# Two-layer graph convolution: raw gathers issued with the degree count's steps, and own-row products moved one group of sums earlier

## The chip, the cores and the metric

The kernel runs on one core of a Trainium2 chip. A core has a matrix engine (PE, with its weight loads shown as PEld), a vector engine (DVE), a scalar engine (ACT), a general engine (POOL, which here issues the indirect gathers) and SP, whose queue issues the plain loads and stores. All of them run side by side and wait for one another through semaphores. The metric is the device time of one execution in microseconds; smaller is better.

## The reference

The input is a table `x` of 6250 rows with 512 values, and 100000 edges `src -> dst` sorted by `dst`. Two Chebyshev convolutions run over it, with float32 throughout:

```python
deg  = segment_sum(ones(E), src, N)                 # how often a node is a source
dinv = where(deg > 0, rsqrt(max(deg, 1)), 0)
norm = -dinv[src] * dinv[dst]
conv = lambda h, W0, W1, b: h @ W0 + segment_sum(h[src] * norm[:, None], dst, N) @ W1 + b

h = relu(layernorm(x))
h = layernorm(conv(h, W1_0, W1_1, b1)) * gamma + beta
h = where(h >= 0, h, 0.01 * h)
out = x + conv(h, W2_0, W2_1, b2)
```

Each convolution thus needs, for every edge, the 512 values of its source row (2 KB), summed over the edges of one destination. `h @ W0` is called the own-row product below; the other product is that of the sums.

## The kernel before

**Chunks, units, groups, blocks.** The edges are cut into 782 chunks of 128 edges. Three chunks make a unit and four units a group, so a group of sums is 12 chunks; there are 66 groups in a layer, and group 0 has only one unit. The nodes are cut into 49 blocks of 128 rows. A chunk is gathered by one indirect DMA on POOL: 128 rows of 2 KB by the column of source indices `sidx[:, t]`. PE then multiplies it by a 0/1 selection matrix (`sel`, made by DVE in `choose`), which sums the edges of equal destination (`sums`, line 706), and ACT copies the group's sum to `agg` (line 721). Since the edges are sorted, a block's sums lie in about three successive groups. `inside[i]` names them, and `inside[i].stop` is the group in whose turn block `i` is finished. For the first blocks these stops are 3, 4, 6, 7, 8, 10, 11, 12, 14: three blocks for every four groups.

**Finishing a block.** `turn` (line 829) transposes the block's own rows `h` (`own`, line 596, four transposes, and an ACT copy to `hT`, line 598), places the groups' sums into the block (`place`, line 742) and scales them into `an` with ACT (line 841). `first_half` (line 845) transposes `an`, has DVE copy it to `aT` (line 851), and meanwhile does the own-row products from `hT` into a new PSUM tile `u_ps` (line 608). `second` (line 859) adds the products of the sums from `aT` and calls `finish`: on DVE a layer norm in layer 0 and a few sums in layer 1 (lines 804 to 824), then the store. Up to group 53 `second` of a block waits in the list `left` until the next group's turn. `hT` has one buffer; `u_ps` and `hT_ps` have two each.

**Order.** In the main loop (lines 932 to 1078) the instructions of PE, POOL and SP are issued in the order in which the code has them. Those of DVE and ACT are put in order by a planner. On PE a group's turn reads: `second` of the block left over, `own`, `place`, the sums of the group, `first_half`.

**Slots.** A gathered chunk lies in a slot until its sums are done. `ring` (line 46) gives the slots out: 12 are lent by the weights and biases, which arrive later, and 63 are the places where `x` lay; 8 of these go to later weights, so that from chunk 75 on 55 places are used in turn. Chunk 130 is therefore written to the slot of chunk 75, the first chunk of group 7, and its gather waits for the sums of group 7. All chunks after it have such a predecessor too.

**Before the main loop.** SP loads `x` (groups of 2, 4, 4, 4, 7, 7, 7, 7, 7 blocks) into the places. ACT takes the statistics and turns each block in place into `relu(layernorm(x))` (line 306), and SP stores it to a table in DRAM, `tab[0]` (line 307). A place is free for a gather when its block is stored. At the same time DVE and PE count the degrees: 25 steps `g` (line 379), in each of which DVE makes two one-hot tables `lo` and `hi` (line 382) for PE. Steps 1, 4, 7, 11, 17 and 21 also finish a part of the table (`turns`, line 355): 2, 4, 4, 4, 7 and 7 blocks. The first 76 chunks are gathered "raw", from `x` itself rather than from the table: 75 of them by `gather_raw` (line 268), of which the first 26 need no stored block (12 lent slots and 14 spare places), and the others one freed place each, in order. ACT scales raw chunks later (line 576), by factors that the `look_up` steps find.

Of the kernel before, what the change touches and what calls it, by code (L numbers as in the profile page):

```python
# [34 lines left out]
AHEAD_OF = 27  # L35
JOIN = 12
WIDE = 35
NARROW = 26
# [24 lines left out]
def gnn_kernel(  # L63
# [203 lines left out]

    def gather_raw(lo, hi):
        for t in range(lo, min(hi, X + RE + NB)):
            nc.gpsimd.indirect_dma_start(  # L270
                out=lent[t] if t < X else places[:, t - X, :D], out_offset=None, in_=x,
                in_offset=bass.IndirectOffsetOnAxis(ap=sidx[:, t : t + 1], axis=0))

    gather_raw(0, X + RE)

# [24 lines left out]
    def make_table(i0, n):  # L300

        for lo in range(i0, i0 + n, 2):
            hi = min(lo + 2, i0 + n)
            for i in range(lo, hi):
                v = places[:, RE + i, :D]
                nc.scalar.activation(v, v, AF.Relu, bias=nb_all[:, i : i + 1], scale=rs_all[:, i : i + 1])
            nc.sync.dma_start(tab[0][lo * P : hi * P, :].rearrange("(i p) d -> p i d", p=P),
                              places[:, RE + lo : RE + hi, :])
            gather_raw(X + RE + lo, X + RE + hi)

# [51 lines left out]
    with tc.tile_pool(name="deg", bufs=1) as dp, tc.tile_pool(name="onehot", bufs=2) as ohp, tc.tile_pool(  # L362
# [15 lines left out]
        for g in range(EJ // (2 * GJ)):  # L378
            hot = []
            for s, n, name in ((s_lo, LO, "lo"), (s_hi, HI, "hi")):  # L380
                t = ohp.tile([EP, GJ, n, 2], BF, name=name)
                nc.vector.tensor_tensor(  # L382
                    t, s[:, g * 2 * GJ : (g + 1) * 2 * GJ].rearrange("p (j s) -> p j s", s=2)[:, :, None, :]
                    .to_broadcast([EP, GJ, n, 2]),
                    iota_c[:EP, None, :n, :].to_broadcast([EP, GJ, n, 2]), op=OP.is_equal)
                hot.append(t.rearrange("p j n s -> p j (n s)"))
            k = turns.get(g)
            if k is not None:
# [63 lines left out]
def usual_path(tc, have):  # L452
# [19 lines left out]
    with ExitStack() as es:  # L472
# [273 lines left out]
        def end_matrices():  # L746
# [3 lines left out]
            nc.vector.tensor_scalar_add(at, iota_r[:, :r], 1.0 + END * P)  # L750
            ps = psum.tile([P, D], F32, name="u_ps")[:, :r]
            nc.tensor.matmul(ps, ones.to_broadcast([P, P]), own_row.pop(0)[:, :r], start=True, stop=True)
# [76 lines left out]
        def turn(layer, i, left=()):  # L829
# [4 lines left out]
            if i + AHEAD < NB:  # L834
                load(layer, i + AHEAD)
            hT = None if i in EARLY else own(layer, i)
            for k, aT in left:
# [7 lines left out]
        def first_half(layer, i, hT, an, between=None):  # L845
# [26 lines left out]
        def check():  # L872
# [12 lines left out]
            for at, num in ((1, min(D, NC - 1)), (1 + D, NC - 1 - D)):  # L885
                if num > 0:
                    ps = psum.tile([P, D], F32, name="u_ps")[0:1, :num]
                    nc.tensor.matmul(ps, ident[:, 0:1], dlx[:, at + 1 : at + 1 + num], start=True, stop=False)
# [17 lines left out]
            for j, (lo, hi) in enumerate(halves):  # L906
                up = pool.tile([P, D], F32, name="xt")[:, : P - 1]
                nc.vector.tensor_sub(up, ident[:, 1:], ident[:, : P - 1])
                ps = psum.tile([P, D], F32, name="u_ps")[: P - 1, : hi - lo]
                nc.tensor.matmul(ps, up, dlx[:, 1 + lo : 1 + hi], start=True, stop=True)  # L910
# [3 lines left out]
                yield  # L914
            ps = psum.tile([P, D], F32, name="u_ps")[0:1, 0:1]
            for j in range(2):
# [15 lines left out]
        for layer in range(2):  # L932
# [5 lines left out]
            for g in range(NS - 1):  # L938
# [469 lines left out]
```

## Time and profile before

| | |
|---|---|
| median of 3 runs | 2024.12 us (2021.15 to 2028.18) |
| profiled execution | 2021.31 us, of which the span from the first to the last instruction is 2019.4 us |
| granted TensorE clock, mean | 0.92 |
| PE busy | 1665.2 us, 82% of the span |
| POOL busy | 1489.1 us, 74% |
| DVE busy | 681.6 us, 34% |
| ACT busy | 389.0 us, 19% |
| DMA | 510.33 MB, 253 GB/s over the span |

A page of the profile shows one execution. It gives each engine's busy time, the groups of instructions by source line (count, mean length, and what ended the idle time before them), and the chain of work that ended last. Other views of the same trace list the instructions in order of time, sum the busy time of each engine in chosen stretches, or sum who waited for whom. In the last two, "issue" stands for time in which an engine waited for nothing that the profile shows. The releaser that is named is the last event before the start; where the idle time is the usual one between two instructions, that engine did not wait for it.

### The profile page before, as it was taken

The numbers are of one execution on the slowest core, as the hardware profiler recorded it, in microseconds if no ns is written. First come the engines' busy times: TensorE is split into PE (matmuls) and PEld (weight loads), VectorE is DVE, ScalarE is ACT, GpSimd is POOL, SyncE is SP. The second block draws the span as 40 slices with busy tenths as digits, with TensorE's granted clock in tenths as the row PEclk, the third lists the DMA queues.
The fourth block names the chain that finished last, engine by engine and source line by source line (L and its number), as shares of the span: only waits on it lengthen the run. The fifth ranks groups of instructions, "written<-read, shape, count | busy, mean of one in ns | idle before, by whom it ended". The sixth has DMA issues, their size and how long they took to land.

```text
span 2019.4 us, 19064 instructions
## 1 busy us (share of the span) xinstructions
PE 1665.2 (82%) x6850; PEld 663.2 (33%) x6850; DVE 681.6 (34%) x1454; ACT 389.0 (19%) x703; POOL 1489.1 (74%) x1578
## 2 busy tenths in 40 slices
PE   5589998677887776888888888888888888888898
PEld 4444443222333222333323322223322323333333
DVE  8975453323244233343352111122111211112221
ACT  7895221111111111111111011011010101011110
POOL 5477777777777777777777777777777777777774
PEclk9889999888998888999999999989999999989999
DMA  9998888887888887888877887787777778788875
GB/s 334 392 376 258 249 252 247 239 241 238 269 248 242 241 243 231 252 258 242 252 237 242 244 255 243 236 247 246 228 243 243 244 234 240 230 253 262 273 234 173
DMA packets 180278, 510.33 MB, mean 253 GB/s; under 512 B 33615, under 2 KB 35389, under 8 KB 180173
## 3 DMA queue, kind: packets, MB, share of 16 engines
q0 software_dynamic: 125120, 415.88, 68.5%
q1 hardware_dynamic: 55013, 93.12, 12.9%
q8 instruction: 56, 0.92, 0.2%
q14 instruction: 49, 0.40, 0.1%
q10 hardware_dynamic: 40, 0.02, 0.0%
HBM read 470.01 MB, written 38.86 MB: 252 GB/s over the span
## 4 chain that ended last, share of the span: by engine, by line
POOL 39%; PE 21%; DMA 17%; issue 16%; DVE 5%; ACT 2%; POOLq 0%; DVEq 0%; SPq 0%; ACTq 0%
POOL places L515 39%; DMA places<-tab,sidx 12%; PE u_ps L608 10%; PE ps L706 6%; PE an_ps L742 3%; DMA places<-tab,lidx 2%; ACT places L576 1%; DVE lo L382 1%; DVE hi L382 1%; PE hT_ps L849 1%; DMA dst_c<-in_dst_dram 1%; DMA places<-in_x_dram,sidx 1%; PE hT_ps L596 1%; DMA tab<-places 1%; DVE st L813 0%
## 5 line engine op out<-in xcount | busy, mean ns | idle before, releaser
L515 POOL DMA_INDIRECT places<-tab,sidx x1191 | 1130.1, 949 | 364.1 <-issue 327.5
L706 PE MATMUL ps<-places,sel 128*32 128x512 f32 x3104 | 511.0, 667 | 143.1 <-DMA places<-tab,sidx 86.6
L742 PE MATMUL an_ps<-agg,there 128*128 128x512 f32 (+1 forms) x554 | 268.6, 617 | 95.8 <-ACT agg L721 91.8
L515 POOL DMA_INDIRECT places<-tab,lidx x270 | 255.5, 946 | 82.3 <-issue 78.9
L706 PEld LDWEIGHTS ps<-places,sel 128*32 128x32 f32 x3104 | 102.0, 117 | 519.2 <-issue 194.6
L650 DVE TENSOR_TENSOR sel<-dlx,nodes_ps 128x384 f32<-128x384 f32 (+3 forms) x134 | 72.3, 541 | 417.5 <-PE ps L706 405.6
L608 PE MATMUL u_ps<-w,hT 128*128 128x512 f32 (+1 forms) x400 | 185.4, 607 | 20.7 <-ACT hT L598 20.2
L721 ACT ACTIVATE agg<-ps 128x512 f32<-128x512 f32 (+2 forms) x130 | 76.2, 588 | 610.0 <-PE ps L706 583.5
L608 PE MATMUL u_ps<-places,hT 128*128 128x512 f32 (+2 forms) x408 | 185.4, 598 | 2.9 <-ACT hT L598 2.9
L742 PEld LDWEIGHTS an_ps<-agg,there 128*128 128x128 f32 (+1 forms) x554 | 104.9, 197 | 216.8 <-issue 108.3
L608 PE MATMUL u_ps<-w,aT 128*128 128x512 f32 x384 | 173.1, 593 | 3.1 <-DVE aT L851 3.1
L608 PE MATMUL u_ps<-places,aT 128*128 128x512 f32 x384 | 173.4, 593 | 0.8 <-DVE aT L851 0.8
L690 DVE TENSOR_TENSOR sel<-sel,places 128x384 f32<-128x384 f32 (+9 forms) x76 | 35.1, 468 | 331.9 <-DMA places<-tab,sidx 331.9
L804 DVE SCALAR_TENSOR_TENSOR u_ps<-u_ps,root,bias 128x512 f32<-128x512 f32 x45 | 34.1, 758 | 284.8 <-PE u_ps L608 284.8
L598 ACT ACTIVATE hT<-hT_ps 128x512 f32<-128x512 f32 (+1 forms) x98 | 58.2, 594 | 291.3 <-PE hT_ps L596 290.9
L608 PEld LDWEIGHTS u_ps<-w,hT 128*128 128x128 f32 (+1 forms) x400 | 73.7, 194 | 96.7 <-issue 74.8
L608 PEld LDWEIGHTS u_ps<-places,hT 128*128 128x128 f32 (+1 forms) x408 | 75.7, 196 | 78.5 <-issue 73.6
L816 ACT ACTIVATE sd<-mv,eps 128x1 f32<-128x1 f32 (+1 forms) x49 | 14.4, 294 | 441.1 <-DVE mv L814 441.1
L270 POOL DMA_INDIRECT places<-in_x_dram,sidx x63 | 59.6, 947 | 52.6 <-ACT junk L286 19.0
L729 DVE TENSOR_SCALAR there<-iota_r,node_of 128x128 f32<-128x128 f32 (+1 forms) x286 | 68.2, 307 | 89.4 <-PE an_ps L742 89.4
L608 PEld LDWEIGHTS u_ps<-w,aT 128*128 128x128 f32 x384 | 70.7, 190 | 83.2 <-issue 78.6
L608 PEld LDWEIGHTS u_ps<-places,aT 128*128 128x128 f32 x384 | 70.6, 190 | 80.3 <-issue 78.3
(200 smaller groups left out, 1245.3 us busy)
## 6 DMA issues: line engine op xcount, KB each, us to landing
places<-tab,sidx POOLq DMA_INDIRECT x1191, 3.8
h<-tab SPq DMA_DIRECT2D x70, 256.0 KB
xt<-in_x_dram SPq DMA_DIRECT2D x48, 256.0 KB
out_dram<-t SPq DMA_DIRECT2D x48, 256.0 KB
tab<-places SPq DMA_DIRECT2D x22, 528.0 KB
places<-in_x_dram SPq DMA_DIRECT2D x5, 1792.0 KB
tab<-t SPq DMA_DIRECT2D x26, 256.0 KB
tab<-places SPq DMA_DIRECT2D x20, 256.0 KB
```

The costliest lines, as they stand in the source:

```text
L270: nc.gpsimd.indirect_dma_start(out=lent[t] if t < X else places[:, t - X, :D], out_offset=None, in_=x, in_offset=bass.IndirectOffsetOnAxis ...
L382: nc.vector.tensor_tensor(t, s[:, g * 2 * GJ : (g + 1) * 2 * GJ].rearrange("p (j s) -> p j s", s=2)[:, :, None, :] .to_broadcast([EP, GJ, ...
L515: nc.gpsimd.indirect_dma_start(out=places[:, slot(t), :] if own_scale else zr(layer, t), out_offset=None, in_=x if layer == 0 and t < RAW ...
L598: nc.scalar.activation(hT[:, :, :r], ps[:, :, :r], AF.Copy)
L608: nc.tensor.matmul(u_ps[:r], hT[:, kc, :r], w[:, kc, :], start=(start and kc == 0), stop=(stop and kc == KD - 1))
L650: nc.vector.tensor_tensor(sel[:, q : q + k, :w, :], of, node[:, q : q + k, None, :].to_broadcast([P, k, w, Q]), op=OP.is_equal)
L690: last = nc.vector.tensor_tensor(v, v, places[:, k : k + hi - lo, D : D + 1].to_broadcast([P, hi - lo, Q]), op=OP.mult)
L706: members.append(nc.tensor.matmul(to, sel[:, q, s, :], rows_of, start=(s == 0), stop=(s == len(chunk[q]) - 1 and (cnt is None or chunk[q][ ...
L721: nc.scalar.activation(agg[g][: n * Q, lo : lo + w], ps[: n * Q, lo : lo + w], AF.Copy)
L729: behind[1] = nc.vector.tensor_scalar(t[:m, :r], iota_r[:m, :r], node_of[:m, g : g + 1], -(1.0 + i * P), op0=OP.subtract, op1=OP.is_equal)
L742: all_of.append(nc.tensor.matmul(placed[i][:r], t[:m, :r], agg[g][:m, :], start=(g == inside[i][0]), stop=(g == inside[i][-1])))
L804: nc.vector.scalar_tensor_tensor(v, v, root[:r, i : i + 1], bias2[:r], op0=OP.mult, op1=OP.add)
```

## The change

Two things are changed, and one name follows from them.

First, `gather_raw` no longer issues the 26 raw gathers at once. Four are issued as before. Each degree step `g` up to 15 then opens one or two more, which wait for that step's `hi` table on DVE, until 26 are open at step 15. Step 16 opens those of the places freed by then (14), and from there each pair of stored blocks opens its own two gathers, as before. All raw gathers keep their order.

Second, a block that is finished in the next group's turn gets its own transposes and its own-row products in the present group: the transposes behind the sums and ahead of `first_half` of the block that is due, the products behind that `first_half`. In layer 0 this holds for groups 6 to 51, in layer 1 for groups up to 51. `turn` and `first_half` then leave them out. Third, the tiles of `end_matrices` and `check` take the PSUM name `hT_ps` instead of `u_ps`.

```diff
+FIRST = 4
+SPREAD = 16
...
-    def gather_raw(lo, hi):
-        for t in range(lo, min(hi, X + RE + NB)):
-            nc.gpsimd.indirect_dma_start(
-                out=lent[t] if t < X else places[:, t - X, :D], out_offset=None, in_=x,
-                in_offset=bass.IndirectOffsetOnAxis(ap=sidx[:, t : t + 1], axis=0))
-
-    gather_raw(0, X + RE)
+    raw, issued, begun = FIRST, 0, []
+
+    def gather_raw(after=None):
+        nonlocal issued
+        while issued < min(raw, X + RE + NB):
+            t = issued
+            with ExitStack() as order:
+                if begun:
+                    order.enter_context(tc.issue_after(begun[-1].ins))
+                got = nc.gpsimd.indirect_dma_start(
+                    out=lent[t] if t < X else places[:, t - X, :D], out_offset=None, in_=x,
+                    in_offset=bass.IndirectOffsetOnAxis(ap=sidx[:, t : t + 1], axis=0))
+            begun.append(got)
+            if after is not None:
+                tc.add_manual_dep(got.ins, after.ins.name,
+                                  mybir.DependencyInfo(mybir.DependencyClass.Sync, mybir.DependencyReason.DATA),
+                                  reason="row gathers are spread over the degree count")
+            issued += 1
+
+    gather_raw()
+    freed = [0]
+
+    def open_to(t, after=None):
+        nonlocal raw
+        raw = t
+        gather_raw(after)
...
-            gather_raw(X + RE + lo, X + RE + hi)
+            freed[0] = hi
+            if issued >= X + RE:
+                open_to(X + RE + hi)
...
-                nc.vector.tensor_tensor(
+                made = nc.vector.tensor_tensor(
...
+            if g < SPREAD:
+                open_to(FIRST + (g + 1) * (X + RE - FIRST) // SPREAD, made)
+            elif g == SPREAD:
+                open_to(X + RE + freed[0])
...
-            hT = None if i in EARLY else own(layer, i)
+            hT = None if i in EARLY or i in started else own(layer, i)
...
-            if i not in EARLY:
+            if i not in EARLY and i not in started:
                 started[i] = psum.tile([P, D], F32, name="u_ps")
                 products(started[i], hT, w_late[:, 1] if layer else w_sb[1], rows[i], True, False)
...
+                ahead_of = (g < NS - JOIN - 2 and inside[i].stop <= g + 1 and len(due) < 2
+                            and (layer == 1 or g >= SOON.stop))
+                if ahead_of:
+                    next_hT = own(layer, i)
                 for k, (hT, an) in due:
                     if g < NS - JOIN:
                         left.append((k, first_half(layer, k, hT, an)))
                     else:
                         dense(layer, k, hT, an)
+                if ahead_of:
+                    started[i] = psum.tile([P, D], F32, name="u_ps")
+                    products(started[i], next_hT, w_late[:, 1] if layer else w_sb[1], rows[i], True, False)
```

More of the change, by code (lines that the diff above doesn't have):

```diff
@@ L750, in end_matrices @@
             nc.vector.tensor_scalar_add(at, iota_r[:, :r], 1.0 + END * P)
-            ps = psum.tile([P, D], F32, name="u_ps")[:, :r]
+            ps = psum.tile([P, D], F32, name="hT_ps")[:, :r]
             nc.tensor.matmul(ps, ones.to_broadcast([P, P]), own_row.pop(0)[:, :r], start=True, stop=True)
@@ L886, in check @@
                 if num > 0:
-                    ps = psum.tile([P, D], F32, name="u_ps")[0:1, :num]
+                    ps = psum.tile([P, D], F32, name="hT_ps")[0:1, :num]
                     nc.tensor.matmul(ps, ident[:, 0:1], dlx[:, at + 1 : at + 1 + num], start=True, stop=False)
@@ L908, in check @@
                 nc.vector.tensor_sub(up, ident[:, 1:], ident[:, : P - 1])
-                ps = psum.tile([P, D], F32, name="u_ps")[: P - 1, : hi - lo]
+                ps = psum.tile([P, D], F32, name="hT_ps")[: P - 1, : hi - lo]
                 nc.tensor.matmul(ps, up, dlx[:, 1 + lo : 1 + hi], start=True, stop=True)
@@ L914, in check @@
                 yield
-            ps = psum.tile([P, D], F32, name="u_ps")[0:1, 0:1]
+            ps = psum.tile([P, D], F32, name="hT_ps")[0:1, 0:1]
             for j in range(2):
```

## The prediction

> **What bounds the kernel now.** I read the page's head first, then the stretches, then POOL's instructions in order of time, because the first two point there.
>
> ```profile
> span 2019.4 us, 19064 instructions
> POOL 39%; PE 21%; DMA 17%; issue 16%; DVE 5%; ACT 2%; POOLq 0%; DVEq 0%; SPq 0%; ACTq 0%
> ...
> 40.00:60.00 20.00, 13.12 (x113) 11.53 (x111) 19.96 (x18) 19.46 (x48) 2.87 (x4) 0.83 0.91 328
> 60.00:80.00 20.00, 12.06 (x115) 10.74 (x114) 20.00 (x18) 18.18 (x43) 7.51 (x8) 0.91 1.04 395
> 240.00:300.00 60.00, 60.00 (x268) 24.39 (x270) 31.19 (x72) 13.54 (x24) 45.57 (x48) 1.00 0.83 250
> 300.00:400.00 100.00, 76.15 (x326) 29.46 (x318) 34.76 (x78) 14.84 (x27) 75.65 (x80) 0.90 0.81 243
> 1800.00:1900.00 100.00, 90.69 (x342) 36.40 (x344) 23.75 (x50) 12.34 (x20) 75.62 (x81) 0.95 0.84 268
> ```
>
> The columns of a stretch are its length, then busy time and count of PE, PEld, DVE, ACT and POOL, the granted clock, the DMA share and GB/s. POOL issues 80 gathers in 100 us at 300 us and 81 at 1800 us: one per 1.25 us. The waits of POOL say that this is its own pace:
>
> ```profile
> POOL places L515 <- issue: 406.7, 1335, 0.3
> POOL places L515 <- ACT pre L721: 1.4, 1, 1.4
> ```
>
> Of its main gathers 1335 started 0.3 us after the one before, waiting for nothing. The busy time of 0.95 us and this 0.3 us make the 1.25 us. In the whole main loop one idle time stands out, the 1.4 us of the second row. So the kernel is a chain on POOL: 1564 gathers (2 x 782) of 1.25 us are 1955 us of the 2019.4 us. PE and DMA have room in nearly all stretches, and PE work only matters where it holds a gather. Time is lost where POOL stands still:
>
> ```profile
> 36.91 0.95 POOL L270 DMA_INDIRECT places<-in_x_dram,sidx  x1 [0.30 <-issue]
> 47.98 0.94 POOL L270 DMA_INDIRECT places<-in_x_dram,sidx  x1 [10.13 <-ACT junk L286]
> 58.71 0.94 POOL L270 DMA_INDIRECT places<-in_x_dram,sidx  x1 [8.53 <-ACT junk L286]
> 82.75 0.95 POOL L270 DMA_INDIRECT places<-in_x_dram,sidx  x1 [0.30 <-issue]
> 88.67 0.94 POOL L270 DMA_INDIRECT places<-in_x_dram,sidx  x1 [4.98 <-DMA tab<-places]
> ...
> 200.90 1.02 POOL L515 DMA_INDIRECT places<-tab,sidx  x1 [0.30 <-issue]
> 203.33 0.94 POOL L515 DMA_INDIRECT places<-tab,sidx  x1 [1.41 <-ACT pre L721]
> ...
> L515 POOLq EVENT_SEMAPHORE  x2: 17/3412/6807, 195.8 to 203.1; - x2
> ...
> 1021.12 0.95 POOL L526 DMA_INDIRECT places<-tab,eidx  x1 [0.31 <-issue]
> L526 POOLq EVENT_SEMAPHORE  x7: 17/43/6075, 1013.2 to 1046.5; - x7
> ...
> 2000.90 0.94 POOL L515 DMA_INDIRECT places<-tab,lidx  x1 [0.30 <-issue]
> ```
>
> The first 26 gathers are out at 37.9 us. Up to 88.67 us POOL waits for stored blocks and issues only 14 more; from there it never stops. The one later stop is chunk 130 at 203.33 us. POOL's queue met its wait at 195.8 us and was held for 6.807 us, to 202.6 us; without it the gather would have begun at 200.90 + 1.02 + 0.30 = 202.2 us. Its slot is that of chunk 75, so it waits for the sums of group 7. PE shows that they end just then:
>
> ```profile
> 186.53 2.76 PE L706 MATMUL ps<-places,sel 128*32 128x512 f32 x18 [1.84 <-ACT places L576]
> 189.23 0.66 PE L849 MATMUL hT_ps<-ident,an 128*128 128x128 f32 x4
> 189.72 3.60 PE L608 MATMUL u_ps<-w,hT 128*128 128x512 f32 x8
> 193.16 0.60 PE L596 MATMUL hT_ps<-ident,h 128*128 128x128 f32 x4
> 193.59 3.60 PE L608 MATMUL u_ps<-w,aT 128*128 128x512 f32 x8
> 197.03 1.02 PE L742 MATMUL an_ps<-agg,there 128*128 128x512 f32 x2
> 199.70 2.78 PE L706 MATMUL ps<-places,sel 128*32 128x512 f32 x24
> 212.88 2.78 PE L706 MATMUL ps<-places,sel 128*32 128x512 f32 x24
> ```
>
> The row at 186.53 is the rest of group 6, that at 199.70 is group 7, ending at 202.48, and that at 212.88 is group 8. Between groups 6 and 7 PE has no gap. So the start of POOL's last unbroken run, and with it the end of the kernel, is set by PE at this one place. The second queue wait of note (6.075 us at 1013.2) ends at 1019.3 us, ahead of its gather at 1021.12.
>
> **The change part by part.**
>
> **Own rows ahead, at group 6.** Blocks 2 and 3 stop at 6 and 7, so group 6 is the first in layer 0 to work ahead. Block 3's transposes move from 193.16 to behind the sums of group 6; both places lie ahead of group 7's sums, so they cost nothing. Block 3's own-row products move from behind group 7's sums (the same kind of row as the one at 189.72) to ahead of them. PE is full here, so they delay those sums by the pitch of that row, 193.16 - 189.72 = 3.44 us.
>
> There is a second piece. `hT` has one buffer. Block 3's copy into it must wait until block 2's products, which end at 189.72 + 0.44 (the transposes put ahead) + 3.44 = 193.6 us, have read the old content, and block 3's products follow directly on PE. The length of that copy:
>
> ```profile
> 193.85 0.60 ACT L598 ACTIVATE hT<-hT_ps 128x512 f32<-128x512 f32 x1 [3.92 <-PE hT_ps L596]
> ```
>
> It is 0.60 us, and it begins 0.1 us after the transposes that end at 193.76; with as much again for the way back to PE I take 0.85 us. Before, this copy lay under the `second` of the block left over. The bounds are 0 (the copy hidden after all) and 1.5 us (ACT late by one more copy of this length). Sum of the piece: 3.44 + 0.85 = 4.3 us, bounds 3.4 to 4.9. Group 7's sums end at 206.8 instead of 202.5, and chunk 130 goes out at 203.33 + 4.3 = 207.6 us.
>
> On this bubble the Trainium skill has a rule (Perfetto Trace Analysis, Optimization Strategy): the same gap repeating on a busy engine can mean that there is no buffer for the next tile. By that rule the sum is 4.3 us; without a bubble it would be 3.4. No run here shows the bubble yet; the one buffer is in the code.
>
> **The groups after it.** Group 8 is pushed likewise: its sums end at 212.88 + 2.78 + 4.3 = 220.0, with up to 0.5 us more for the copy, which now has only `first_half`'s transposes as cover. The gather that needs them (chunk 142) is twelve behind chunk 130, at 207.6 + 15.0 = 222.6 us. Margin some 2 us. At group 8 no block is worked ahead (stop 10 follows stop 8), so PE gives 3.44 us back there. From 300 us on PE is idle for a fifth of the time (76.15 of 100), the moved products fall partly into that, and POOL does not see them. `u_ps` now holds two blocks at once; the older must be through DVE's `finish` before the next products:
>
> ```profile
> 210.41 0.70 DVE L810 TENSOR_TENSOR u_ps<-u_ps,bias 128x512 f32<-128x512 f32 x1 [5.94 <-PE u_ps L608]
> 214.47 0.75 DVE L824 SCALAR_TENSOR_TENSOR t<-u_ps,dinv,t 128x512 f32<-128x512 f32 x1
> ```
>
> That is 4.8 us, against 2.67 (`place`) + 2.71 (sums) + 0.44 + 0.49 (transposes) = 6.3 us of PE work in between: covered by 1.5 us. It is uncovered where DVE waits for a gather, which happens when PE has caught up with POOL, and there no slot is short: 0.
>
> **The rest of layer 0, the turn of the layers, layer 1.** From group 52 on the order is unchanged. The wait at 1013.2 is for layer 0's last blocks, which follow the gathers; it moves with them: 0, bounds -1 to +2. In layer 1 POOL keeps 81 gathers per 100 us; the moved products fill PE's idle time. After the last gather at 2000.90 the tail of 18.5 us is unchanged. The tiles that move to `hT_ps` are few, and short against the room on PE: 0.
>
> **The raw gathers.** The 22 gathers are not removed, only put later. They wait for DVE:
>
> ```profile
> 60.40 1.78 DVE L382 TENSOR_TENSOR hi<-s_hi,iota_w 125x3136 bf16<-125x3136 bf16 x1
> ```
>
> This is step 15, ending at 62.2 us. Gathers 24 and 25 follow it, then the 14 of the freed places: the sixteenth starts 15 x 1.25 us after 62.9, at 81.7 us. Before, the same gather went out at 82.75. So POOL has lost nothing by then, if the blocks are stored in time. The next one waited for a stored block until 88.67 us. DMA is full in this stage (0.91 and 1.04 of 1), so what the gathers leave early, loads and stores take; by 82 us both versions have moved the same. I expect it between 82.9 us (POOL's pace) and 94 us (as much later as it could be earlier), and take 88.67. In either case it is hidden: POOL must be at chunk 130 by 206.9 us (its wait then ends) and would be there at 202.2 us, so it may slip 4.7 us before it counts, and being early gains nothing. Term: 0, bounds 0 to +0.7.
>
> No instruction of DVE waits for POOL in the degree count, so its steps keep their times. SP's order is unchanged.
>
> **Sum.** 4.3 + 0 + 0 = +4.3 us, against the profiled execution's 2021.31 (the span of 2019.4 and 1.9 us around it): 2025.6. That execution is 2.8 us below the median of the runs, 2024.12; so the median to expect is 2028.4, say 2028 us, or +0.2%. About 0.3%, 6 us, is what a measurement of this kernel tells from no change (the three runs spread by 7 us), so this is "within 0.3%", near its edge.
>
> **The rivals.**
>
> *Slower by more, through the stores.* If the burst of 14 gathers from 62.9 to 82 us takes DMA's share just when the blocks of step 17 are stored, gather 40 comes late. It decides above 88.67 + 4.7 = 93.4 us. How far it can go: SP issues that store at 75.84 us, and it landed 12.8 us later.
>
> ```profile
> 75.84 37.49 SPq L307 DMA_DIRECT2D tab<-places  x20
> ```
>
> At double that, 101.5 us, the whole stream is 12.8 late and the kernel 4.3 + 12.8 - 4.7 = 12.4 us slower: 2036. Against it: before that burst loads and stores have had DMA more to themselves. The Trainium skill (DMA: Bandwidth & Descriptors, SWDGE vs HWDGE vs iDMA) says that each DMA engine takes turns between the gathers' queue and the others, so stores would not stand behind a run of gathers; no run here shows that apart. Chance 0.15.
>
> *Slower by more, on PE.* If ACT or DVE are put in another order by the planner, so that block 3's copy or the scaling ahead of group 6 (the 1.84 us gap at 186.53) comes later, every us counts in full. With 3 us more: 2031. Chance 0.2.
>
> *No cost.* If the copy and the products find room (group 6's sums later held by something else), the gate stays at 202.6 us: 2024, no change. Chance 0.1.
>
> *Faster.* For this the sums of group 7 would have to end earlier and POOL to be there earlier; the first alone gains 1.1 us. With gather 40 at 82.9 us and PE's chain before group 7 shortened by as much, 5.8 + 1.1 = 6.9 us: 2017. Nothing in the change shortens that chain. Chance 0.07.
>
> **How the numbers follow.** The forecast has 0.48. Slower by over 0.3% (above 2030.2): the two slower rivals and a small part of the forecast, 0.37. Faster: 0.07. Within: 0.56. The likeliest one's own range is 2024 to 2032 (bounds of the sum and some 3 us of scatter in a median); with the rivals 2020 to 2036.
>
> **What would show it.** Right: chunk 130's gather (the first main gather with a gap over 2 us) near 207.6, PE with two rows of eight own-row products between the sums of groups 6 and 7 and a gap of some 0.85 us between them, 80 gathers per 100 us after it, and a tail of 18.5 us. The raw gathers stand in the steps up to 62 us and run on from there. Wrong: gather 40 past 93 us, a second stop of POOL at chunk 142 or at the turn of the layers, or group 7's sums ending before 204 us.

## The result, and the profile after

Over 20 runs of each kernel the changed one takes 2027.51 us in the median (2025.95 to 2030.61), the kernel before 2024.27 us (2020.99 to 2028.18). The ratio is 1.0019, with a 95% interval of 1.0013 to 1.0025. So the change costs 3 to 4 us: a small loss, clear of the noise, and inside the forecast of 2028 us and "within 0.3%". The profiled execution of the changed kernel takes 2027.51 us, its span is 2025.7 us; against the profiled execution of before that is 6.2 us more.

POOL's gathers in order of time, in the changed kernel (start, length, instruction, and in brackets the idle time before it):

```profile
59.85 0.94 POOL L279 DMA_INDIRECT places<-in_x_dram,sidx  x1 [1.89 <-DVE hi L405]
...
77.21 0.94 POOL L279 DMA_INDIRECT places<-in_x_dram,sidx  x1 [2.67 <-DMA tab<-places]
...
81.42 0.95 POOL L279 DMA_INDIRECT places<-in_x_dram,sidx  x1 [0.30 <-issue]
89.07 0.94 POOL L279 DMA_INDIRECT places<-in_x_dram,sidx  x1 [6.71 <-ACT root L446]
...
200.62 0.94 POOL L542 DMA_INDIRECT places<-tab,sidx  x1 [0.30 <-issue]
210.72 0.94 POOL L542 DMA_INDIRECT places<-tab,sidx  x1 [9.16 <-ACT pre L748]
...
2006.93 0.94 POOL L542 DMA_INDIRECT places<-tab,lidx  x1 [0.30 <-issue]
```

From gather 40 on (89.07 us) chunk 130 is still the one place where POOL stands for more than half a us, now for 9.16 us instead of 1.41. It goes out at 210.72 instead of 203.33 us, 7.4 us later. The last gather is 6.0 us later (2006.93 against 2000.90), the span 6.2 us longer. What POOL waits for in the main loop has not changed otherwise:

```profile
POOL places L542 <- issue: 408.2, 1340, 0.3
...
POOL places L542 <- ACT pre L748: 9.5, 2, 9.2
```

The later stretches show the same pace as before, 80 gathers in 100 us at 300 us and 81 at 1800 us, and show one stretch that differs, at 140 us, where the granted clock is 0.83, and 1.00 in the kernel before (columns: length, busy time and count of PE, PEld, DVE, ACT and POOL, granted clock, DMA share, GB/s):

```profile
140.00:160.00 20.00, 15.89 (x69) 8.15 (x73) 6.95 (x15) 10.25 (x16) 15.12 (x17) 0.83 0.98 351
...
300.00:400.00 100.00, 79.54 (x334) 31.30 (x326) 36.01 (x81) 15.31 (x28) 75.94 (x80) 0.90 0.82 244
1800.00:1900.00 100.00, 87.57 (x341) 33.64 (x334) 23.09 (x49) 11.56 (x19) 75.62 (x81) 0.97 0.84 263
```

PE shows where the 7.4 us come from. First its instructions in the changed kernel:

```profile
149.16 6.04 PE L635 MATMUL u_ps<-w,hT 128*128 128x512 f32 x8 [3.22 <-DMA w<-in_L_gnn_W_dram]
...
158.18 2.78 PE L733 MATMUL ps<-places,sel 128*32 128x512 f32 x24
...
189.47 2.76 PE L733 MATMUL ps<-places,sel 128*32 128x512 f32 x18 [1.84 <-ACT places L603]
192.17 0.66 PE L623 MATMUL hT_ps<-ident,h 128*128 128x128 f32 x4
192.66 0.60 PE L876 MATMUL hT_ps<-ident,an 128*128 128x128 f32 x4
193.10 3.60 PE L635 MATMUL u_ps<-w,hT 128*128 128x512 f32 x8
197.44 3.70 PE L635 MATMUL u_ps<-w,hT 128*128 128x512 f32 x8 [0.75 <-ACT hT L625]
200.98 3.60 PE L635 MATMUL u_ps<-w,aT 128*128 128x512 f32 x8
...
207.08 2.78 PE L733 MATMUL ps<-places,sel 128*32 128x512 f32 x24
...
211.20 3.70 PE L635 MATMUL u_ps<-w,hT 128*128 128x512 f32 x8 [0.31 <-ACT hT L625]
...
220.84 2.78 PE L733 MATMUL ps<-places,sel 128*32 128x512 f32 x24
```

and the two rows of the kernel before that answer to the first two, from the same view:

```profile
148.63 3.66 PE L608 MATMUL u_ps<-w,hT 128*128 128x512 f32 x8
...
155.27 2.78 PE L706 MATMUL ps<-places,sel 128*32 128x512 f32 x24
```

The sums of group 7 start at 207.08 instead of 199.70 us, 7.38 later, and chunk 130 follows them at the same distance as before (3.64 against 3.63 us). The 7.38 us are two pieces:

- **4.44 us between groups 6 and 7.** The rest of group 6's sums is 2.94 us late (189.47 against 186.53), those of group 7 are 7.38 late. In between stand two rows of eight own-row products instead of one, with a gap of 0.75 us at 197.44 us that ends with the copy to `hT`. This is the piece that the prediction worked out.
- **2.94 us before group 6.** They are there at group 4 already (158.18 against 155.27 us). Block 0's own-row products waited 3.22 us for the second weight, and then the eight ran for 6.04 instead of 3.66 us, while the granted clock of the stretch fell to 0.83. This piece the prediction did not have. It is a difference between two single executions; the experiments show how far it belongs to the change.

ACT's row for that copy shows that it waits in turn for the products that read the old content of the one buffer:

```profile
196.79 0.60 ACT L625 ACTIVATE hT<-hT_ps 128x512 f32<-128x512 f32 x1 [3.92 <-PE u_ps L635]
```

### The profile page after: what moved, and what is told of

The parts are those of the page before. It is cut to its first block, busy times and chain, and to the rows that moved or that the text cites. A ratio compares the mean times of both kernels' runs of the same rounds, so it can differ in the third digit from the quotient of the medians.

```text
span 2025.7 us, 19127 instructions
## 1 busy us (share of the span) xinstructions
PE 1660.9 (82%) x6850; PEld 672.7 (33%) x6850; DVE 684.9 (34%) x1454; ACT 388.1 (19%) x703; POOL 1488.4 (73%) x1578
## 5 line engine op out<-in xcount | busy, mean ns | idle before, releaser
L733 PE MATMUL ps<-places,sel 128*32 128x512 f32 x3104 | 473.2, 636 | 108.6 <-DMA places<-tab,sidx 69.9
L635 PE MATMUL u_ps<-w,hT 128*128 128x512 f32 (+1 forms) x400 | 210.7, 675 | 138.8 <-ACT hT L625 135.1
L769 PE MATMUL an_ps<-agg,there 128*128 128x512 f32 (+1 forms) x554 | 255.6, 595 | 4.3 <-DVE rs L846 4.3
L635 PEld LDWEIGHTS u_ps<-w,hT 128*128 128x128 f32 (+1 forms) x400 | 81.9, 216 | 237.1 <-ACT hT L625 144.9
L868 ACT ACTIVATE an<-an_ps,ndeg 128x512 f32<-128x512 f32 x45 | 30.9, 687 | 343.7 <-PE an_ps L769 343.7
L837 DVE TENSOR_TENSOR u_ps<-u_ps,bias 128x512 f32<-128x512 f32 x45 | 31.3, 696 | 174.3 <-PE u_ps L635 174.2
```

Of the source, the lines that this page charges most:

```text
L635: nc.tensor.matmul(u_ps[:r], hT[:, kc, :r], w[:, kc, :], start=(start and kc == 0), stop=(stop and kc == KD - 1))
L733: members.append(nc.tensor.matmul(to, sel[:, q, s, :], rows_of, start=(s == 0), stop=(s == len(chunk[q]) - 1 and (cnt is None or chunk[q][ ...
L769: all_of.append(nc.tensor.matmul(placed[i][:r], t[:m, :r], agg[g][:m, :], start=(g == inside[i][0]), stop=(g == inside[i][-1])))
L837: nc.vector.tensor_add(v, v, pre.pop(i)[:r] if i in EARLY else bias1[:r])
L868: nc.scalar.activation(an[:r], placed.pop(i)[:r], AF.Copy, scale=(ndeg if layer == 1 and i not in EARLY else ndinv)[:r, i : i + 1])
```

## The experiments

The first four ran side by side, with runs of the kernel before on the same chip (2025.91 us in the median of 35). Whether the result came from this chip too is not known; the kernel before took 2024.27 us there, 0.1% less, and both are called the first chip below. What the profiles show at the gate, against the kernel before, can be put in one table. All are us; a shift is a start (or the end of the span) minus that in the profile of the kernel before. That profile is of one of the shortest executions (2021.31 us, median 2024.27), so a shift of 2 or 3 us can be scatter; the column of differences is not touched by this.

| kernel | rest of group 6 | sums of group 7 | difference | chunk 130 | end of span |
|---|---|---|---|---|---|
| changed | +2.94 | +7.38 | 4.44 | +7.39 | +6.2 |
| gathers spread only | -0.71 | -0.72 | -0.01 | +2.02 | +0.2 |
| own rows ahead only | +0.94 | +5.38 | 4.44 | +5.39 | +5.0 |
| ahead from group 9 on | +2.25 | +2.24 | -0.01 | +2.24 | +2.2 |
| weights in order of use | +1.76 | +6.20 | 4.44 | +6.20 | +5.6 |

**Spread alone.** The changed kernel without the own rows ahead:

```diff
-                ahead_of = (g < NS - JOIN - 2 and inside[i].stop <= g + 1 and len(due) < 2
-                            and (layer == 1 or g >= SOON.stop))
+                ahead_of = False
```

> The raw gathers are spread as in the changed kernel, no own rows are worked ahead. Theory (the sums of group 7 hold chunk 130, and that alone sets the end): the 4.4 us of the moved products go, the 2.9 us that PE lost to the late weights stay; chunk 130 near 206.3 us instead of 210.7, median 4.4 us below the changed kernel, about 2023, which is -1 us (-0.05%) against the kernel before, or up to +2.9 us where the weights are as late as in the profiled execution. Rival (the late raw gathers cost POOL its start): the whole +3.2 us of the change stays, median 2027.5.

Measured: 2023.39 us (2018.51 to 2026.46, 11 runs), ratio 0.9993, interval 0.9983 to 1.0003. POOL and PE in this run:

```profile
137.64 0.94 POOL L542 DMA_INDIRECT places<-tab,sidx  x1 [4.05 <-ACT places L603]
...
205.35 0.95 POOL L542 DMA_INDIRECT places<-tab,sidx  x1 [0.30 <-issue]
```

```profile
185.82 2.76 PE L733 MATMUL ps<-places,sel 128*32 128x512 f32 x18 [1.84 <-ACT places L603]
...
198.98 2.78 PE L733 MATMUL ps<-places,sel 128*32 128x512 f32 x24
```

The spread gathers cost nothing that can be measured. PE's sums of group 7 are even 0.72 us earlier, so the 2.9 us of late weights that were expected to stay did not, with the same spread gathers. Chunk 130 goes out without a wait. It does so 2.0 us later than before all the same, because POOL itself had been stopped at 137.64 us, at chunk 76, the first that is read from the table. So here the stop at chunk 76 sets the run of gathers, and PE at group 7 does not. The spread is not shown to be its cause: the next run, without it, has the same stop, 4.04 us long, and the whole change has none (0.30 us).

**Own rows ahead alone.** The kernel before with the second part of the change and the renamed tiles:

```diff
+                ahead_of = (g < NS - JOIN - 2 and inside[i].stop <= g + 1 and len(due) < 2
+                            and (layer == 1 or g >= SOON.stop))
+                if ahead_of:
+                    next_hT = own(layer, i)
...
+                if ahead_of:
+                    started[i] = psum.tile([P, D], F32, name="u_ps")
+                    products(started[i], next_hT, w_late[:, 1] if layer else w_sb[1], rows[i], True, False)
```

> Own rows are worked ahead as in the changed kernel, the raw gathers go out at once as before. Theory: chunk 130 at 203.3 + 4.3 = 207.6 us, no wait for weights at block 0, +4.3 us (+0.21%) against the kernel before, median about 2028.5. Rival (the late raw gathers are the cost): no change against the kernel before, 2024.3, and chunk 130 at 203.3 us. Second rival (the spreading gains what PE's earlier degree count gains, 2.6 us, and the change hides it): slower than the changed kernel by up to 2.6 us, 2030.

Measured: 2029.08 us (2026.33 to 2035.47, 12 runs), ratio 1.0019, interval 1.0009 to 1.0029, the same as the whole change. PE, then POOL:

```profile
187.47 2.76 PE L708 MATMUL ps<-places,sel 128*32 128x512 f32 x18 [1.84 <-ACT places L578]
...
195.44 3.70 PE L610 MATMUL u_ps<-w,hT 128*128 128x512 f32 x8 [0.75 <-ACT hT L600]
...
205.08 2.78 PE L708 MATMUL ps<-places,sel 128*32 128x512 f32 x24
```

```profile
139.15 0.94 POOL L517 DMA_INDIRECT places<-tab,sidx  x1 [4.04 <-ACT places L578]
...
208.72 0.94 POOL L517 DMA_INDIRECT places<-tab,sidx  x1 [2.18 <-ACT pre L723]
```

The gap of 0.75 us and the 4.44 us are there again, with the gathers as they were before. The second part of the change carries its whole cost; the 2.94 us ahead of group 6 are 0.94 here, and the ratio is the same.

**Ahead from group 9 on.** The changed kernel, in which layer 0 works ahead only from group 9 on, so that block 3 (and the block after it) keeps its old place and all later ones are ahead:

```diff
-                            and (layer == 1 or g >= SOON.stop))
+                            and (layer == 1 or g >= SOON.stop + 3))
```

> The changed kernel, but in layer 0 own rows are worked ahead from group 9 on, not from group 6: 2 of some 34 blocks of that layer are put back. Theory (one place decides): the whole cost of working ahead goes; chunk 130 near 206.3 us, median like that of the spread gathers alone, some 4.4 us below the changed kernel, about 2023. Rival (each block worked ahead costs PE a gap for the one hT buffer or for u_ps, and the gaps add up): at least nine tenths of the cost stay, 2027.

Measured: 2023.57 us (2021.51 to 2027.59, 11 runs), ratio 0.9988, interval 0.9978 to 0.9998. PE, then POOL:

```profile
141.88 0.63 PE L623 MATMUL hT_ps<-ident,h 128*128 128x128 f32 x4 [4.02 <-DMA h<-tab]
142.44 2.07 PE L769 MATMUL an_ps<-agg,there 32*128 32x512 f32 x2
144.44 2.08 PE L769 MATMUL an_ps<-pre,there 128*128 128x512 f32 x2
...
188.78 2.76 PE L733 MATMUL ps<-places,sel 128*32 128x512 f32 x18 [1.84 <-ACT places L603]
...
201.94 2.78 PE L733 MATMUL ps<-places,sel 128*32 128x512 f32 x24
```

```profile
205.57 0.94 POOL L542 DMA_INDIRECT places<-tab,sidx  x1 [3.97 <-ACT pre L748]
```

The 4.44 us are gone, and with them the loss; the kernel is even 0.12% faster than before, by an interval that just leaves out 1. So the dozens of blocks that are worked ahead later, in both layers, cost nothing, and the two at groups 6 and 7 cost everything. In this profile 2.24 us from before group 6 stay: PE had waited 4.02 us for block 0's own rows. The ratio below 1 says that these 2.24 us against one profile of the kernel before are not a loss against its median.

**Weights in the order of use.** The extra 2.94 us of the changed kernel stood behind the second weight, which block 0's own-row products need first. Here it is loaded ahead of the other:

```diff
-        for t, w in zip(w_sb[k - 3 : k - 2], (W1_1, W1_0)[k - 3 :]) if k >= 3 else ():
+        for t, w in zip(w_sb[4 - k : 5 - k], (W1_1, W1_0)[4 - k :]) if k >= 3 else ():
```

> The changed kernel, but the weight that the own-row products read is loaded first and that of the sums second. Theory: PE's wait of 3.2 us for the weights ahead of block 0's own-row products goes, and with it the lower clock after it (5.9 us for eight products instead of 3.5); sums of group 4 and all after them 5.8 us earlier than in the changed kernel, at most, if the other weight is there in time; chunk 130 at 205 to 207 us instead of 210.7; median 3.5 to 5.8 us below the changed kernel, 2022 to 2024. Rival (the wait lies in one execution only, or PE is held by another thing there): no change, 2027.5, and chunk 130 past 209 us.

Measured: 2026.43 us (2023.57 to 2032.09, 12 runs), ratio 1.0006, interval 0.9998 to 1.0015. By the ratios (1.0006, and 1.0019 for the whole change) the gain is some 2.6 us, where 3.5 to 5.8 were expected; the two were not run side by side, and their intervals overlap. In the profile chunk 130 goes out at 209.53 us, past the 209 us that the rival had named. PE:

```profile
143.07 0.63 PE L623 MATMUL hT_ps<-ident,h 128*128 128x128 f32 x4 [3.42 <-DMA h<-tab]
...
144.68 2.08 PE L769 MATMUL an_ps<-pre,there 128*128 128x512 f32 x2
...
150.40 3.17 PE L635 MATMUL u_ps<-w,hT 128*128 128x512 f32 x7
...
205.90 2.78 PE L733 MATMUL ps<-places,sel 128*32 128x512 f32 x24
```

The wait for the weight is gone (150.40 us has none), but PE now waits 3.42 us for block 0's own rows, which are loaded in the same stage, and 1.76 of the 2.94 us remain. So the order of the weights is not shown to be the cause of the 2.94 us. What PE waits for here differs from one profile to the next: the second weight (3.22 us in the changed kernel, 0.53 with the gathers spread only, 0.21 with own rows ahead only), or block 0's own rows (3.42 and 4.02 us).

**Four kernels on a second chip.** The next four were to test the gates themselves. In the kernel before with `SOON` to group 7 (both blocks due at groups 6 and 7 finished behind the sums), the gate at group 7 should open:

```diff
-    SOON = range(3, 6)
+    SOON = range(3, 8)
```

> The kernel before, with `SOON` reaching to group 7: the blocks due in groups 6 and 7 are finished behind the sums of the same group, so their products leave the path ahead of group 7's sums. Theory (the start of POOL's last unbroken run sets the end, and in the kernel before that is the sums of group 7): those sums end some 7 us earlier, chunk 130 goes out at POOL's own pace, 202.2 instead of 203.33 us, and the time falls by 1.1 us, ratio 0.9995. Rival (PE's work in this stage counts in full): 7 us less, ratio 0.9965. Rival (the pile is only put off): a later group stops POOL, at chunk 142 or 154, and the time is the same or longer.

In the kernel before without the second load of one group of `x` (the first part of the table, `k = 0`, calls `load_rest(-1)`, so that `groups[5]` is loaded twice):

```diff
-                if k < 4:
+                if 1 <= k < 4:
                     load_rest(k - 1)
```

> The kernel before, without the second load of one group of seven blocks of `x` that degree step 0 issues (1.84 MB that are loaded twice). At the 390 GB/s of this stage that is 4.7 us of DMA time. Theory (DMA bounds the stage from 40 to 90 us, and the sums of group 7 hold chunk 130): gather 40 comes some 4 us earlier, at 84 to 85 us; chunk 130 comes earlier only by what PE's groups 3 to 7 come earlier, 0 to 4 us, through the loads that PE waits for; ratio 0.998 to 1.000. Rival (POOL alone sets the time): 4.5 us less, ratio 0.9978. Rival (the second load lies in idle DMA time): nothing moves, 1.000.

The changed kernel with both of these edits, the weights in the order of use, and own rows ahead from group 9 on (two of its four edits are shown):

```diff
+    SOON = range(3, 8)
...
+                            and (layer == 1 or g >= SOON.stop + 1))
```

> The changed kernel with four edits: `SOON` to group 7, the own rows ahead from group 9 on in layer 0, the weights of the first layer loaded in the order of their use, and no second load of the group of `x`. Theory (POOL's run from gather 40 on is then held by nothing, if PE's groups come in time): gather 40 at 83 to 84 us, chunk 130 at 197 to 199 us, the time 4 to 6 us below the kernel before, ratio 0.997 to 0.998. Rival (the load that PE waits for at block 0 or the stored table at chunk 76 stops POOL once more): chunk 76 or chunk 130 waits, and the ratio is 0.999 to 1.000.

And the kernel before with the first two edits, `SOON` to group 7 and no second load:

> The kernel before with two edits: `SOON` to group 7 and no second load of the group of `x`. Theory: the two are more than their sum, because either gate alone hides the other: gather 40 at 84 to 85 us and no stop at chunk 130, so 4 to 5.5 us below the kernel before, ratio 0.9973 to 0.998. Rival (a later wait, for the table at chunk 76 or for PE at a later chunk, takes the place): 0 to 2 us less, ratio 0.999 to 1.000.

On this chip the kernel before itself took 2399.1 us (2385.41 to 2413.34, 29 runs), 18% more than on the first. Measured, in this order: ratio 0.9999 (0.9977 to 1.0021), 0.9998 (0.9974 to 1.0022), 0.9930 (0.9906 to 0.9954) and 0.9999 (0.9979 to 1.0019). No theory had a kernel that is bound as this one is: behind chunk 130 POOL stops for more than 0.6 us at 93 to 102 gathers in the four profiles, nearly once in every group of 12 chunks, and at none in the kernel before on the first chip. So a gate at chunk 130 decides nothing. What the four were to tell of the first chip stays open. But one result asked for an answer: the kernel that holds the change was 0.7% faster.

**Once more, with the changed kernel itself.** Three of the four and the changed kernel as it is were run again, side by side; they fell on a third chip, where the kernel before took 2378.79 us (2363.67 to 2390.88, 24 runs).

> The changed kernel as it is, beside the same runs of the kernel before as the three that follow. In the run of the four kernels before this one, the kernel before took 2399 us instead of 2024, with idle time on all engines that the profile ties to no event. If that returns: theory (working ahead gives PE work while it would stand) 0.993 to 0.998; rival (the 0.7% that the combined kernel gained there came from its other edits) 0.999 to 1.001. If the kernel before takes 2024 us again: 1.0019, chunk 130 at 207 to 211 us, as measured.

> The kernel before with `SOON` reaching to group 7, once more. Where the kernel before takes some 2024 us. Theory (the sums of group 7 set the start of POOL's last unbroken run, by 1.1 us): chunk 130 goes out near 202.2 us without a wait, ratio 0.9995. Rival (PE's work in this stage counts in full): 7 us less, 0.9965. Rival (the pile is put off to chunk 142 or 154): 1.000 or above. Where it takes some 2399 us: 1.000, as measured.

> The changed kernel with `SOON` to group 7, own rows ahead from group 9 on in layer 0, the weights in the order of their use and no second load of one group of `x`, once more. Where the kernel before takes some 2024 us. Theory: gather 40 at 83 to 84 us, nothing stops POOL from there to chunk 130 at 197 to 199 us, ratio 0.997 to 0.998. Rival (the load that PE waits for or the stored table at chunk 76 stops POOL once more): 0.999 to 1.000. Where it takes some 2399 us: 0.993, as measured.

> The kernel before with `SOON` to group 7 and no second load of one group of `x`, once more. Where the kernel before takes some 2024 us. Theory (either gate alone hides the other): gather 40 at 84 to 85 us, no stop at chunk 130, 4 to 5.5 us less, ratio 0.9973 to 0.998. Rival (a wait for the table at chunk 76 or for PE at a later chunk takes the place): 0.999 to 1.000. Where it takes some 2399 us: 1.000, as measured.

Measured: the changed kernel 2360.1 us (2356.09 to 2366.69, 6 runs), ratio 0.9916 (0.9892 to 0.9940); the kernel before with `SOON` to group 7 1.0015 (0.9995 to 1.0035); the combined kernel 0.9944 (0.9918 to 0.9970); the kernel before with two edits 1.0022 (1.0000 to 1.0045). So on a chip on which the kernel takes 18% longer, the change is a gain of 0.84%, and no gain of the other edits can be measured. POOL in the changed kernel on this chip:

```profile
88.31 0.94 POOL L279 DMA_INDIRECT places<-in_x_dram,sidx  x1 [8.27 <-DMA tab<-places]
...
251.39 0.95 POOL L542 DMA_INDIRECT places<-tab,sidx  x1 [10.19 <-ACT pre L748]
```

and in the kernel before with `SOON` to group 7:

```profile
99.11 0.95 POOL L270 DMA_INDIRECT places<-in_x_dram,sidx  x1 [13.22 <-ACT ln L292]
...
255.35 0.95 POOL L515 DMA_INDIRECT places<-tab,sidx  x1 [4.43 <-ACT pre L721]
```

The wait at chunk 130 is there, 10.19 us long, and it does not decide: chunk 130 comes 4.0 us earlier in the changed kernel than in the other, in spite of it, and the end 17.9 us earlier (spans 2364.9 and 2382.8). The stretch that tells most about the own rows lies late in layer 0, from gather 500 to gather 612 (their slots wait for the sums of groups 37 to 47, and layer 0 works ahead up to group 51). It takes 161.4, 162.7 and 162.8 us in the three runs of kernels that work ahead, and 167.6 to 171.7 us in the five that do not. In this stretch the gathers of the degree count are long past, which points to the own rows ahead. From gather 612 to 782, where layer 0 works nothing ahead, the two kinds no longer differ (260.9 to 261.5 against 261.0 to 265.3). From gather 130 to 300 it is 240.2 to 245.3 us against 246.0 to 251.5; between 300 and 500 the two kinds lie within each other (285.4 to 289.5). On the first chip the stretch from 500 to 612 took 140.6 us before and 140.0 us after: POOL's own pace, and nothing to gain.

The other part of the change acts on these chips too, and far more than on the first. With the gathers issued at once (here in the kernel with `SOON` to group 7), DVE stood in the degree count until 42.01 us, 3.8 us after the last of the 26 had been issued:

```profile
42.01 1.22 DVE L382 TENSOR_TENSOR lo<-s_lo,iota_w 125x2048 bf16<-125x2048 bf16 x1 [19.31 <-remote]
```

In the changed kernel the same table is made 21.6 us earlier, without a wait:

```profile
20.46 1.21 DVE L405 TENSOR_TENSOR lo<-s_lo,iota_w 125x2048 bf16<-125x2048 bf16 x1
```

Step 15 follows at 80.0 to 80.8 us in the five profiles with the gathers at once and at 56.7 to 58.7 in the three with spread ones; on the first chip these are 59.6 to 60.4 and 56.1 to 57.8. At gather 40 some 11 us of it are left (88.31 against 99.11), at gather 130 the 4.0 us named above. The other 13.9 of the 17.9 us come later, 9.9 of them up to gather 782. The kernel before was not profiled on the third chip, and the two parts of the change were not run apart on it, so how the gain divides between them is not shown.

## Why the prediction was right, and where it was not

**What bounds the kernel: right, on the chip of the profile.** In the kernel before and in the four others of the table in which chunk 130 waits, it follows the sums of group 7 at 3.63 to 3.64 us. The end follows chunk 130 less closely: the shift at the end is 0.1 to 1.2 us smaller in the four. The spread-only run shows the limit of it: its sums are early enough, so POOL's own earlier stop takes over, and of a shift of 2.0 us at chunk 130 only 0.2 reach the end.

**Own rows ahead: 4.3 us forecast, 4.44 measured.** The products cost 3.54 us (197.44 to 200.98) against 3.44. The bubble from the one `hT` buffer is 0.90 us by the starts of the rows (197.44 - 193.10 - 3.44), of which the record shows 0.75 as idle, against 0.85. The own transposes moved within the same stretch at no cost, as worked out. Here the Trainium skill's rule (Perfetto Trace Analysis, Optimization Strategy), by which a repeating gap on a busy engine can mean a missing buffer for the next tile, came out: 0.75 us in the three profiles that work ahead at group 6, and 0.31 us at group 7 (211.20 us). That the first groups alone pay is shown by the run that works ahead from group 9 on. The times that were named came 3.1 us late all the same (chunk 130 at 210.72 instead of 207.6 us), by the piece ahead of group 6.

**The groups after it, the rest and layer 1: right.** Group 8's sums are 7.96 us late (220.84 against 212.88), 0.58 more than group 7's, where up to 0.5 more was allowed. No second stop came at chunk 142, 80 and 81 gathers per 100 us stayed, and the turn of the layers, costed at 0 with bounds of -1 to +2, gave 1.1 us back (the shift against before is 7.27 us at gather 782 and 6.16 us at gather 815). One reading was too kind: PE is idle for a quarter of the stretch at 300 us (76.15 of 100 us busy) but for only a tenth at 1800 us (90.69), not for a fifth throughout. It did no harm, since POOL kept its pace.

**The raw gathers: 0 is right, the way to it was not.** The spread-only run bears out the 0 (ratio 0.9993). Gather 39 was forecast at 81.7 and came at 81.42 us, gather 40 at 88.67 and came at 89.07. But "its steps keep their times" failed: step 15 came 2.6 us earlier.

```profile
57.80 1.78 DVE L405 TENSOR_TENSOR hi<-s_hi,iota_w 125x3136 bf16<-125x3136 bf16 x1
```

In the kernel before this row stands at 60.40 us. The step comes earlier in every profile with spread gathers (56.1 to 57.8 us, against 60.40 and 59.62 us without), so the spread moves it; that the first loads land earlier with fewer gathers in the way is the likely reason, and not shown apart. So gather 24 went out at 59.85 instead of 62.9 us, and the run of sixteen would have ended at 78.6 us; two waits (2.67 us for a store and 0.76 us, instead of the usual 0.30) put it back to 81.42. Two errors cancelled; that the number fits is luck.

**What was missing: where the 2.6 us went, and 2.94 us more.** The prediction had said of PE's chain before group 7 that "Nothing in the change shortens that chain". It is shortened in its first part, but PE then meets loads that land no earlier: DMA is full in that stage (share 1.04 from 100 to 140 us), and block 0's own rows and weights stand in it. Then comes the slow stretch of PE described below. Against the profile of before this is a loss of 1.8 to 2.9 us in three profiles, and -0.7 and +0.9 us in the two others; the kernel with the gathers spread only (-0.7) and the one that is ahead from group 9 on (+2.2) have the same code up to there. So the piece is not shown to belong to the change, and single executions differ by 3 us in it. The medians speak against it too: they stand 3.2 us apart, which leaves no room for 4.44 and 2.94 us, and the run from group 9 on is not slower than the kernel before although its gate is 2.24 us late. More likely the profile of before caught an execution in which these loads came in time. The profiled execution is 6.2 us above that of before, 4.3 were forecast; that the forecast of the median fits better (2028 against 2027.51 us) is in part luck, since the profile of before lay 3 us below its median and that of after on it.

**The rivals.** The late stores did not come (gather 40 at 89.07 us, the bound was 93.4). "No cost" fell with the 4.44 us. "Slower by more, on PE" did come in the profile, by the 3 us that it named, but not in the median (2031 was named), and not by the cause that it named: the 1.84 us gap ahead of group 6's rest is 1.84 us as before, and the delay entered at block 0. "Faster" was given 0.07 on the chip of the profile, which is fair there; that another chip can turn the sign was not thought of at all.

## What to carry to other kernels

Look for the one place where the bounding engine still waits, and cost a moved step there and not on average: the blocks worked ahead at groups 6 and 7 made up the whole loss here, and starting a few groups later removes it. A chain that starts 2 to 4 us earlier gained at most 0.7 us here, where the next thing that it needs is a load in a stage in which DMA is full. Compare medians before explaining a shift between two single profiles. And a forecast from one profile holds for a chip that behaves as in that profile: the same change cost 0.2% on one chip and gained 0.8% on another.

## What the runs showed of the hardware

**PE at half its clock around block 0.** Behind the 3.22 us wait at 149.16 us eight products took 6.04 us instead of 3.66. The stretches of the changed kernel show the granted clock at half there (columns as above):

```profile
147.00:149.00 2.00, 0.00 (x0) 0.00 (x0) 0.20 (x1) 2.00 (x4) 1.69 (x2) 0.52 1.04 369
149.00:153.90 4.90, 4.74 (x6) 2.16 (x7) 0.00 (x0) 0.29 (x1) 3.69 (x4) 0.50 1.04 401
```

In the kernel before it is 1.00 in both. Behind 4.02 us two placements took 2.07 and 2.08 us, and behind 3.42 us one took 2.08, where 1.12 is their usual length (at 143.72 us in the kernel before). In the two profiles in which the wait for the weight was 0.53 us or less the products kept 3.70 us. So in the changed kernel the late load cost its wait and 2.4 us more. The Trainium skill (TensorE: Matmul & The Clock Gate, Part 1: The HAM clock gate) has the clock fall to half after an idle window of some 3.4 us. The three profiles agree in kind. The length of the wait alone is no threshold here: by the record the clock is at half from 147.1 us, when PE had stood for 1.1 of its 3.22 us, and behind the 3.42 us it fell only 1.5 us after the wait.

**Two other chips, on which what follows PE's sums starts late.** There the kernel takes 18% longer at almost the same number of instructions. Each chip was used at one time only, so whether this belongs to the chips or to the hour is not shown. By the record PE's instructions have nearly their usual lengths (573 ns in the mean in the kernel with `SOON` to group 7, 562 in the kernel before on the first chip), but what follows them starts late. PE, ACT and POOL in the kernel with `SOON` to group 7 on the third chip:

```profile
1812.84 2.78 PE L706 MATMUL ps<-places,sel 128*32 128x512 f32 x24
```

```profile
1823.64 0.60 ACT L721 ACTIVATE agg<-ps 128x512 f32<-128x512 f32 x1 [16.56 <-remote]
```

```profile
1823.88 0.95 POOL L515 DMA_INDIRECT places<-tab,sidx  x1 [2.44 <-remote]
```

The sums end at 1815.62 us by the record, their copy by ACT begins 8.0 us later, and POOL goes on 0.24 us after ACT, as if the same signal had released both. Over the 132 groups of both layers the time from the recorded end of the sums to the copy is 0.14 us in the median on the first chip, in both kernels, and 3.45 (changed kernel) and 3.65 us (kernel with `SOON` to group 7) on the third. The profile ties the waits to nothing on this core. These are the groups of waits for that copy on the third chip, and on the first in the kernel before:

```profile
ACT agg L721 <- remote: 497.1, 56, 27.8
```

```profile
ACT agg L721 <- PE ps L706: 583.5, 107, 17.8
```

The Trainium skill (Perfetto Trace Analysis, Tensor Engine Instruction) says that the end of a matmul in the records is an estimate, and that the signal to the other engines goes out after it. By that PE's work may in truth have ended later than shown. The starts of PE's instructions speak against a slower array, since what follows 24 sums on PE starts as close behind them as on the first chip (2.72 us at 1812.84 us, 2.71 at 199.70 us there). The cause stays open.

That the whole change gains there is measured; why it does is argued only: a block's turn has a way from PE to ACT and back (own transposes, copy to `hT`, products), the sums' way to ACT has become longer by 3.3 to 3.5 us, and the change takes one such way out of the turn that finishes the block. The spread gathers, which free the degree count from its wait of 19.31 us, are the other candidate, and no run there tells the two apart.
